# A two-layer transformer kernel: scores for the maxima in three passes, two filler banks, whole PSUM tiles in the planned part

## The chip, the core and the metric

The kernel runs on one core of one Trainium2 chip. The metric is device time in microseconds of one execution, as the median of three runs.

A core has a matrix engine (TensorE, PE in the profile; PEld is its weight load), a vector engine (VectorE, DVE), an activation engine (ScalarE, ACT), GpSimd (POOL) and a queue that starts transfers (SyncE, SP). Matmul results go to PSUM, which the kernel divides into eight banks of 512 fp32 columns on 128 partitions. DVE and ACT take them out from there; the program makes a matmul that writes a bank again wait for the bank's last reader.

## The reference

Input x has 2 x 1024 tokens of width 256. Two layers follow one another, each with attention and a gated FFN beside each other:

```python
xn = _layernorm(x)
x = x + _L0_attn_ref(xn, ...) + _L0_ffn_ref(xn, ...)
xn = _layernorm(x)
x = x + _L1_attn_ref(xn, ...) + _L1_ffn_ref(xn, ...)
```

Layer 0 has linear attention (features elu(q)+1 and elu(k)+1, one 16x16 state per head) and an FFN with ternary weights. Layer 1 has softmax attention with rotary positions, and an FFN whose weights are seen through Hadamard transforms. What matters here is layer 1's attention, 16 heads of width 16 in each of the two batches:

```python
q = apply_rope(q)
k = apply_rope(k)
attn = jnp.einsum('bhqd,bhkd->bhqk', q, k) * scaling
probs = jax.nn.softmax(attn, axis=-1)
out = jnp.einsum('bhqk,bhkd->bhqd', probs, v)
```

The softmax needs the maximum of each row of 1024 scores before the exponentials of that row.

## The kernel before, in words

**The planned part.** Layer 0, the first two layer norms of layer 1, the first heads and the first maxima (`search`, L1180) are not issued as they are written. `Plan` (L158) records each operation with what it needs; `Plan.emit` (L225) then makes a list for PE, DVE, ACT and POOL with costs (`cost`, L340) and with the numbers in `LEADS` (L48), one for each group of operations and engine, which are added to an operation's urgency. A needed element is looked up at a grain (`Pool`, L272): the PSUM pool has grain C = 512, so the list sees the two banks of a two-bank tile as two things. In the wide FFN pieces (`ffn0`, L728) one two-bank tile `pug` holds the up product in bank one and the gate product in bank two, eight fp32r matmuls each; a tanh on ACT reads the first bank.

**The loop** (L1332 on) is issued in the order in which it stands. It goes over 8 units; a unit is four heads of one batch. In unit u the exponentials and weighted sums of unit u and the maxima of unit u+1 are made together. A *burst* (`burst`, L1044) works four row groups of 32 rows of PE at a time. Two groups make scores with keys on partitions for the exponentials, in three passes of 512 columns: high part of q, low part of q, and minus the maximum (`weights_of`, L1100, tile `sce`). The other two make scores with queries on partitions for the next unit's maxima, in two passes of 512 columns (`scores_of`, L1053, tile `scm`). After a burst DVE reduces the two banks of `scm` to maxima (`scores_max`, L1064, one reduction of 1024 columns) and ACT takes the exponentials of the two banks of `sce` (1024 columns, tile `pr`).

A unit has 16 steps of two bursts. I call a *half* the stretch from the first matmul of one burst to that of the next. In the A half of a step the weighted sums of the step before follow the burst (`weigh`, L1121, four groups of columns, tile `po`). In the B half *filler* follows: pieces of the FFNs (`pug`, then `py`), of the Hadamard products (`pw`), of the output projections, the transposes of maxima (`put_peaks`, L1088) and of finished sums (`normalise`, L1136), and, in units 0, 2 and 4, the next heads (`heads_of`, L825): a projection `pqkv`, rotation on POOL and DVE, and transposes `pt` (`lay_out`, L844) that ACT and DVE take out as `qk_hi` and `ql`. `fill` (L1216) issues filler for a share of the filler that is left; `go_on` (L1227) gives out the steps that wait for a place, among them the DVE operations behind a finished `pug`, which come behind the next burst's reduction. The last unit has 16 bursts in which all four groups make scores for exponentials, in three passes.

PSUM: `pair` has two buffers of two banks (for `scm` and `sce`), `bank` has three buffers of one bank for all filler, `po` has one bank. Each burst needs both pairs.

Of the kernel before, what the change touches and what calls it, by code (L numbers as in the profile page):

```python
# [21 lines left out]
P = 128  # L22
# [3 lines left out]
NB = E // P  # L26
# [22 lines left out]
    "norm 0a": (1268, 1283, 1353, 1307),  # L49
    "norm 0b": (1266, 1278, 1247, 1252),  # L50
    "norm 1": (1210, 1162, 1187, 1148),
    "project 0": (1056, 1212, 1220, 1354),
    "project 1": (981, 1355, 1139, 1289),
    "state 0": (594, 645, 635, 642),
    "attend 0": (974, 935, 955, 963),
    "attend 1": (417, 552, 629, 461),
    "wuT0": (1187, 1197, 1154, 1169),
    "wgT0": (1364, 1352, 972, 1039),
    "wdT0": (535, 515, 586, 606),
    "piece 0": (460, 529, 461, 589),  # L60
    "piece 1": (1299, 1282, 1268, 1287),
    "piece 2": (1099, 767, 1229, 1058),
    "piece 3": (965, 967, 900, 942),
    "norm1 0": (889, 872, 881, 927),
    "heads 0": (969, 1023, 971, 1088),
    "norm1 1": (921, 944, 969, 1152),
    "heads 1": (951, 921, 937, 944),
    "search 0": (588, 645, 635, 630),
    "search 1": (692, 602, 631, 644),
    "search 2": (639, 616, 689, 676),  # L70
    "search 3": (1243, 1270, 1288, 1295),
    "norm 2": (568, 534, 523, 547),
    "norm 3": (948, 938, 972, 960),
    "project 2": (654, 696, 637, 632),
    "project 3": (572, 548, 504, 552),
    "state 1": (571, 611, 558, 597),
    "attend 2": (1173, 1369, 1172, 1236),
    "attend 3": (644, 574, 633, 573),
    "piece 4": (906, 1076, 609, 921),
    "piece 5": (1168, 1568, 1476, 1520),  # L80
# [278 lines left out]
def tile_two_layers(ctx: ExitStack, tc: tile.TileContext, a: dict, out: bass.AP):  # L359
# [15 lines left out]
    ps = open_pool(ctx, "ps", 1, C, space=PSUM)  # L375
# [3 lines left out]

    def pair(name):  # L380
        return ps.tile([P, 2, C], F32, tag="pair", name=name, bufs=2)

    def bank(name):
        return ps.tile([P, C], F32, tag="bank", name=name, bufs=3)

    po = ps.tile([P, C], F32, tag="po", name="po", bufs=1)
# [84 lines left out]
    def norm_T(src, dst, pause=0.0):  # L471
# [23 lines left out]
        for k in range(2):  # L495
            pt = bank("pt")
            for j in range(CT):
                tensor.transpose(pt[:, j * P : (j + 1) * P], xn[:, j, k * P : (k + 1) * P], ident)
            yield CT * P * TR, SOON
            (vector.tensor_copy if k else scalar.copy)(dst[:, k, :], pt)  # L500
            yield 0.0


    def ffn(cc, first, second, half_scale, scale, down, before_down):
# [4 lines left out]
        for e in range(NB):  # L509
# [20 lines left out]
            vector.scalar_tensor_tensor(h, pug[:, 1, :], scale(e), act, ALU.mult, ALU.mult)  # L530
            hid.append(h)
            yield 0.0
        before_down()
        for j in range(F // P):
            t = at // P + j
            cols = slice(j * P, (j + 1) * P)
            py = bank("py")[:, 0:D]
            for e in range(NB):
                tensor.matmul(py, lhsT=hid[e][:, cols], rhs=down[:, e, :], start=(e == 0), stop=(e == NB - 1))
                if e < NB - 1:  # L540
                    yield D * COL
            yield D * COL, SOON
            vector.tensor_add(xc[c][:, t, :], py, xc[c][:, t, :])
            yield 0.0
# [183 lines left out]
    def ffn0(cc, before_down, wide=False, by_pool=False):  # L728
# [20 lines left out]
        for e in range(0, NB, step):  # L749
# [25 lines left out]
            else:  # L775
                vector.scalar_tensor_tensor(act, pug[:, 1, :, :], sgd, act, ALU.mult, ALU.mult)
            acts.append(act)
# [3 lines left out]
        py = [bank("py")[:, 0:D] for _ in range(F // P)]  # L781
        for e in range(NB):
            if e == 1 and acts:
                split()
            for j in range(F // P):
                if state.plan and e == 0 and not wide:
                    plan.behind(pug)
                for s in range(2):
                    lhsT = hid[e][s][:, j * P : (j + 1) * P]
                    tensor.matmul(py[j], lhsT=lhsT, rhs=wd[:, e, :], start=(e + s == 0), stop=(e + s == NB))  # L790
                if (e, j) != (NB - 1, F // P - 1):
                    yield 2 * D * PASS
        yield 2 * D * PASS, SOON
        for j in range(F // P):
            t = at0 // P + j
            vector.tensor_add(xc[c][:, t, :], py[j], xc[c][:, t, :])
        yield 0.0
# [27 lines left out]
    def heads_of(b, gg, first=0, last=BT):  # L825
# [28 lines left out]
        def take_out(cols, pt):  # L854
            scalar.copy(thk[:, :, cols], pt)
            vector.tensor_tensor(tl[:, :, cols], pt[:, 0:2, :], thk[:, 0:2, cols], ALU.subtract)

# [9 lines left out]
        for i in range(first, last + 2):  # L867
# [4 lines left out]
            if i >= last:  # L872
                yield 0.0, LAST
                if i == last:
                    split_k(i - 1)
                    yield 0.0, PAIR
                continue
            c, j = divmod(b * BT + i, CT)
# [4 lines left out]
            for k in range(2):  # L883
# [7 lines left out]
                if k == 0:  # L891
                    yield 3 * P * COL
            yield 3 * P * COL, LAST
            if i > first:
                split_k(i - 1)
            yield 0.0, FIRST
# [5 lines left out]
            )  # L902
            cos, sin = (
# [46 lines left out]
    def hadamard_in(name, tag):  # L950
        eff = const.tile([P, 2, E], F32, tag=tag, name=f"eff_{name}")
        had[name] = eff
        for n in range(E // C):
            cols = slice(n * C, (n + 1) * C)
            raw = loaded.pop(0)
            for m in range(2):
# [8 lines left out]
                vector.tensor_scalar_mul(eff[:, m, cols], pw, su_ug[:, m : m + 1])  # L965
                yield 0.0

    def hadamard_down():
        wd1 = const.tile([P, NB, D], F32, tag="wC", name="wd1")
        had["wdT1"] = wd1  # L970
        for n in range(2):
            raw = loaded.pop(0)
            for i in range(2):
# [6 lines left out]
                vector.tensor_copy(wd1[:, e : e + 2, :].rearrange("p k n -> p (k n)"), pw)  # L980
                yield 0.0
# [62 lines left out]
    def burst(scores):  # L1044

        for s in range(max(len(passes) for _, passes in scores)):
            for sc, passes in scores:
                if s < len(passes):
                    tensor.matmul(
                        sc, lhsT=passes[s][0], rhs=passes[s][1], start=(s == 0), stop=(s == len(passes) - 1)  # L1050
                    )

    def scores_of(u, j, sc):  # L1053

        b, g = units[u]
        qt, r = divmod(j, 4)
        kh, p = divmod(r, 2)
        qs, ks = slice(qt * P, (qt + 1) * P), slice(kh * C, (kh + 1) * C)
        return [
            (sc[:, i, :], [(q[b, g][rows[2 * p + i], qs], kk[b, g][rows[2 * p + i], ks]) for q in (qh, ql)])  # L1060
            for i in range(2)
        ]

    def scores_max(u, j, sc):  # L1064
        qt, r = divmod(j, 4)
        kh, p = divmod(r, 2)
        n, t = divmod(qt, CT)
        if (u, n) not in peaks:
            peaks[u, n] = small.tile([P, CT, 2, 4], F32, tag="peak", name="peak")
        peak = peaks[u, n]  # L1070
        vector.tensor_reduce(peak[:, t, kh, 2 * p : 2 * p + 2], sc, AX.X, ALU.max, negate=True)
        if j % 16 == 15:
            nm = small.tile([P, CT, 4], F32, tag="nm", name="nm")
            vector.tensor_tensor(nm, peak[:, :, 0, :], peak[:, :, 1, :], ALU.min)
            if u == 0 and n == 1:
                nms.append(nm)
                return
            split_peaks(nm)
            if u > 0:
                later(2, lambda: put_peaks(u, n))  # L1080
# [7 lines left out]
    def put_peaks(u, n):  # L1088
# [7 lines left out]
        scalar.copy(mx[u][:, n * C : (n + 1) * C], pt)  # L1096
        left[0] -= CT * P * TR / 2
        spent[0] += CT * P * TR / 2

    def weights_of(u, i, p, sc):  # L1100

        b, g = units[u]
        n, r = divmod(i, 16)
        ks, qs = slice(r // 2 * P, (r // 2 + 1) * P), slice(n * C, (n + 1) * C)
        made = []
        for k in range(2):
# [3 lines left out]
                (sc[:, k, :], [(keys, qh[b, g][r, qs]), (keys, ql[b, g][r, qs]), (ones_r[r, :], mx[u][r, qs])])  # L1110
# [25 lines left out]
    def normalise(u, n, oT):  # L1136
# [13 lines left out]
        )  # L1150
        if g == NG - 1:
# [4 lines left out]
    def project(b, n):  # L1156
# [3 lines left out]
        pts = []  # L1160
        for k in range(2):
            pts.append(bank("pt"))
            for j in range(CT):
                tensor.transpose(pts[k][:, j * P : (j + 1) * P], att[b, n][:, j, k * P : (k + 1) * P], ident)
        yield 2 * CT * P * TR, SOON
        scalar.copy(aT[:, 0, :], pts[0])
        vector.tensor_copy(aT[:, 1, :], pts[1])
        yield 0.0
        parts_left[c] -= 1
        last = parts_left[c] == 0  # L1170
        for j in range(CT):
# [3 lines left out]
            vector.tensor_add(xc[c][:, j, :], py, xc[c][:, j, :])  # L1175
            if last:
                sync.dma_start(out=out_d[:, c * CT + j, :], in_=xc[c][:, j, :])
            yield 0.0

    def search(part):  # L1180

        for i in range(STEPS // 4):
            j = part // 2 * 16 + part % 2 * 2 + i // 2 * 4 + i % 2
            sc = pair("sc")
            plan.burst = True
            burst(scores_of(0, j, sc))
            plan.burst = False
            scores_max(0, j, sc)
            yield
# [37 lines left out]
    def go_on(*when):  # L1227
# [3 lines left out]
        if urgent and waits.get(urgent[0], 0) in when:  # L1231
# [73 lines left out]
    l0.close()  # L1305
    late.append(open_pool(ctx, "late", 2))
# [11 lines left out]
    slots = STEPS // 2  # L1318
    to_fill = [slots * (len(units) - 1) + slots / 2]
    pending = []  # L1320

    def slot(weight):
        share = max(left[0], 0.0) / to_fill[0] * weight
        to_fill[0] -= weight
        tick()
        fill(max(share - stage(), 0.0), filler)
        go_on(LAST)

    def keep(u, i, prs):
        pending.append((u, i // 16, i % 16 // 2, prs))  # L1330

    for u in range(len(units) - 1):  # L1332
# [9 lines left out]
        for i in range(0, STEPS, 2):  # L1342
            prs = []
            for p in range(2):
                scm, sce = pair("scm"), pair("sce")
                burst(scores_of(u + 1, i + p, scm) + weights_of(u, i, 1 - p, sce))
                scores_max(u + 1, i + p, scm)
# [93 lines left out]
```

## Time and profile before

| | us |
|---|---|
| median of 3 runs | 916.99 (913.85 to 917.79) |
| profiled execution, its own time | 912.87 |
| its span | 911.1 |
| first burst of the loop starts at | 216.0 |
| last maxima of the loop are reduced from | 845.8 |
| clock granted to PE, mean | 0.998 of full |

PE is busy for 95% of the span, DVE 64%, ACT 48%, POOL 24%. A line of the groups reads: line, engine, operation, out<-in, shapes, count, then busy time in total and mean ns of one, then idle time of the engine just ahead of these instructions and who ended it. All lines stand as L316, the helper through which every operation is issued, so the tile names tell the operations apart. A PE row's fp32 matmul counts as two instructions. In the timeline a row has its start, its length, engine, operation, count and, in brackets, how long the engine had been idle and what it waited for. Weight loads start a matmul: the time of a PEld row is when PE begins with it.

### The profile page before, as it was taken

Reading aid. Unit: us, or ns where it says so; the run is one execution under the profiler, and the core shown is the slowest. Engines: PE = TensorE matmul, PEld = TensorE weight load, DVE = VectorE, ACT = ScalarE, POOL = GpSimd, SP = SyncE. Lnnn points to the kernel's source line nnn. Section 1 sums busy time; section 2 is a strip of 40 time slices with the busy share of each in tenths; the row PEclk is TensorE's granted clock in tenths of the full one; section 3 lists DMA queues with packets and bytes.
Section 4 is the critical chain, followed back from the end, with each engine's and each line's share of the span. In section 5 each row is a group of like instructions: output and inputs, shape, how many; then the busy total and the mean of one; then the engine's idle time right before and its main releaser. Section 6 shows DMA issues by size and latency. Waiting matters only on the chain.

```text
span 911.1 us, 14625 instructions
## 1 busy us (share of the span) xinstructions
PE 868.0 (95%) x6064; PEld 518.4 (57%) x6064; DVE 584.2 (64%) x956; ACT 440.6 (48%) x641; POOL 214.7 (24%) x280
## 2 busy tenths in 40 slices
PE   8988999999989998999999999999999999999997
PEld 5677855676546543555555555555555555555543
DVE  5975557787876687656765656677565666656212
ACT  6534565433655543444544444455344444444563
POOL 2645589432643140004500000054000000000000
PEclk9999999999999999999999999999999999999999
DMA  8200000000000110000000000000000000000001
GB/s 304 75 1 1 2 0 1 1 2 1 1 24 25 47 47 0 1 1 1 1 2 1 1 1 25 1 1 2 24 1 1 1 1 1 1 1 1 1 7 40
DMA packets 11313, 14.77 MB, mean 16 GB/s; under 512 B 1264, under 2 KB 8944, under 8 KB 11248
## 3 DMA queue, kind: packets, MB, share of 16 engines
q1 hardware_dynamic: 11248, 13.85, 4.5%
q8 instruction: 47, 0.77, 0.4%
q14 instruction: 18, 0.15, 0.1%
HBM read 11.75 MB, written 2.10 MB: 15 GB/s over the span
## 4 chain that ended last, share of the span: by engine, by line
PE 69%; DVE 21%; ACT 4%; issue 2%; POOL 2%; DMA 1%; SPq 0%; ACTq 0%; POOLq 0%; DVEq 0%
PE pug L316 19%; DVE peak L316 16%; PE scm L316 16%; PE py L316 12%; PE sce L316 7%; PE pqkv L316 4%; PE pt L316 4%; PE pw L316 2%; PE sc L316 2%; PE po L316 2%; ACT pr L316 1%; ACT act L316 1%; DVE act L316 1%; DMA x<-in_x 1%; PE pq L316 1%
## 5 line engine op out<-in xcount | busy, mean ns | idle before, releaser
L316 ACT ACTIVATE pr<-sce 128x1024 f32<-128x1024 f32 x256 | 260.5, 1024 | 269.3 <-PE sce L316 269.0
L316 DVE TENSOR_REDUCE peak<-scm 128x2 f32<-128x1024 f32 x224 | 274.1, 1223 | 166.1 <-PE scm L316 165.2
L316 PE MATMUL po<-pr,va 128*17 128x512 f32 x1024 | 135.6, 598 | 0.0
L316 PEld LDWEIGHTS scm<-qk_hi 32*128 32x128 f32 x448 | 41.4, 181 | 151.1 <-DVE peak L316 113.6
L316 PE MATMUL sce<-qk_hi 32*128 32x512 f32 x512 | 122.6, 494 | 4.8 <-DVE peak L316 2.4
L316 PE MATMUL scm<-qk_hi 32*128 32x512 f32 x448 | 111.5, 494 | 11.8 <-DVE peak L316 1.0
L316 POOL CAST tops<-nm 128x16 fp32r<-128x16 f32 x16 | 3.4, 212 | 406.9 <-DVE nm L316 406.7
L316 PE MATMUL sce<-ql,qk_hi 32*128 32x512 f32 x512 | 97.0, 392 | 0.0
L316 PE MATMUL sce<-mx,ones_r 32*128 32x512 f32 x512 | 97.0, 391 | 0.1
L316 PE MATMUL scm<-qk_hi,ql 32*128 32x512 f32 x448 | 89.0, 394 | 0.0
L316 DVE SCALAR_TENSOR_TENSOR act<-act,pug 128x256 f32<-128x256 f32 (+1 forms) x112 | 50.8, 453 | 58.2 <-ACT act L316 35.1
L316 PE MATMUL pug<-xnT,eff_wgT 128*128 128x256 f32 x256 | 69.2, 392 | 0.0
L316 PE MATMUL pug<-xnT,eff_wuT 128*128 128x256 f32 x256 | 68.3, 382 | 0.0
L316 PE MATMUL py<-wd,hid 128*128 128x256 f32 x256 | 63.2, 388 | 0.0
L316 POOL TENSOR_TENSOR hid<-act,hid 128x256 fp32r<-128x256 f32 (+1 forms) x48 | 45.9, 956 | 70.1 <-ACT hid L316 42.3
L316 ACT ACTIVATE act<-pug,ws_ug 128x256 f32<-128x256 f32 x64 | 30.4, 475 | 55.4 <-PE pug L316 55.4
L316 PEld LDWEIGHTS pug<-xnT,eff_wgT 128*128 128x128 f32 x256 | 45.5, 189 | 16.6 <-issue 10.7
L316 PEld LDWEIGHTS py<-wd,hid 128*128 128x128 f32 x256 | 46.4, 190 | 14.8 <-issue 8.5
L316 PEld LDWEIGHTS sce<-qk_hi 32*128 32x128 f32 x512 | 45.8, 181 | 15.8 <-ACT pr L316 9.9
L316 PEld LDWEIGHTS pug<-xnT,eff_wuT 128*128 128x128 f32 x256 | 47.9, 190 | 9.8 <-issue 2.6
L316 PEld LDWEIGHTS sce<-mx,ones_r 32*128 32x128 f32 x512 | 46.3, 183 | 11.0 <-ACT mx L316 0.5
L316 ACT ACTIVATE act<-pug,su_half 128x256 f32<-128x256 f32 (+1 forms) x48 | 26.1, 546 | 52.1 <-PE pug L316 44.8
(146 smaller groups left out, 1337.6 us busy)
## 6 DMA issues: line engine op xcount, KB each, us to landing
out<-x SPq DMA_DIRECT2D x16, 128.0 KB, 1.7
x<-in_x SPq DMA_DIRECT2D x3, 512.0 KB, 9.4
both<-in_wuT SPq DMA_DIRECT2D x1, 1024.0 KB, 8.8
both<-in_wgT SPq DMA_DIRECT2D x1, 1024.0 KB, 10.4
wdT<-in_wdT SPq DMA_DIRECT2D x1, 1024.0 KB, 12.6
raw<-in_wdT SPq DMA_DIRECT2D x2, 512.0 KB, 4.2
raw<-in_wgT SPq DMA_DIRECT2D x2, 512.0 KB, 3.9
raw<-in_wuT SPq DMA_DIRECT2D x2, 512.0 KB, 3.4
```

Source lines behind the costliest of these rows:

```text
L316: return call(*map(real, args), **{k: real(v) for k, v in kw.items()})
```

## The change

1. In a burst the two groups that make scores for maxima now use all three pass times: their tile `scm` has three banks (`triple`), one head gets three quarters of 256 keys and the other two (turn about), each in two passes, so five quarters a burst in place of four. A matmul has 512 or 256 columns, since a quarter can lie across a bank's edge or a query block's end. Maxima are taken by two reductions, one for each head, the shorter first; in a unit there are 26 such bursts in 13 steps.
2. The three steps left over in a unit (`LOOKS`) have one burst each, all four groups making scores for exponentials into `sce` and `scf` (two banks of the `triple`). So a unit has 29 bursts in place of 32; the last still has 16.
3. PSUM in the loop: one `pair`, one `triple`, two banks `bank0` and `bank1` for filler, `po`. `bank(name)` takes the bank that was not taken last, unless it is held, and a bank is held from being taken until the operation that reads it last has been issued (`free`). A new pool is opened for this behind the planned part.
4. A halves get filler too (`FIRST_PART` = 0.4 us, behind the weighted sums). The heads' projection moves from ahead of the filler to behind it, just ahead of the next burst, and its DVE additions are issued at once. The FFN's down products and the output projection's transposes take one bank at a time.
5. The planned part sees a PSUM tile as a whole (grain 2C) and has new `LEADS`.

```diff
-    ps = open_pool(ctx, "ps", 1, C, space=PSUM)
+    psum = [open_pool(first, "ps", 1, 2 * C, space=PSUM)]
...
     def bank(name):
-        return ps.tile([P, C], F32, tag="bank", name=name, bufs=3)
...
+        k = 1 - last[0] if 1 - last[0] not in held else last[0]
+        assert k not in held, name
+        last[0] = k
+        held.append(k)
+        t = psum[1].tile([P, C], F32, tag=f"bank{k}", name=name, bufs=1)
...
             if i >= last:
-                yield 0.0, LAST
                 if i == last:
+                    yield 0.0, LAST
                     split_k(i - 1)
                     yield 0.0, PAIR
                 continue
+            yield 0.0, LAST
             c, j = divmod(b * BT + i, CT)
...
+    LOOK = [[(3, 2)[(i + k) % 2] if i < 12 else 2 for i in range(13)] for k in range(2)]
+
+    def look(u, p, i, sc):
+
+        flat = sc.rearrange("p b n -> p (b n)")
+        groups, maxima = [], []
+        for k, parts in enumerate(LOOK):
+
+            first, n = sum(parts[:i]), parts[i]
+            at = 0 if n == 3 or (n == LOOK[1 - k][i] and k == 0) else 2 * C
+            group, g = [], first
+            while g < first + n:
+                qt, a = divmod(g, S // F)
+
+                m = min(first + n - g, S // F - a, 2 - (g - first) % 2)
+                col = at + (g - first) * F
+                group += scores(u, 2 * p + k, qt, a * F, (a + m) * F, flat[:, col : col + m * F])
+                g += m
+            groups.append(group)
+            out_ = peaks_of(u)[:, 2 * p + k, :, :].rearrange("p q n -> p (q n)")[:, first : first + n]
+            maxima.append((out_, flat[:, at : at + n * F].rearrange("p (g n) -> p g n", g=n)))
+
+        def take():
+
+            for out_, in_ in sorted(maxima, key=lambda x: x[1].ids.size):
+                vector.tensor_reduce(out_, in_, AX.X, ALU.max, negate=True)
...
+    LOOKS = [i % 5 < 4 for i in range(2 * BT)]
+    ALONE = 0.4
+    FIRST_PART = 0.4
...
-    for u in range(len(units) - 1):
+    for u in range(len(units)):
...
-        for i in range(0, STEPS, 2):
+        m = 0
+        for i in range(2 * BT):
             prs = []
...
+            if LOOKS[i] and u < len(units) - 1:
+                us = share(1)
+                for p in range(2):
+                    scm, sce = triple("scm"), pair("sce")
+                    groups, take = look(u + 1, p, m, scm)
+                    burst(*weights_of(u, i, 1 - p, sce), *groups)
+                    take()
+                    prs.append(weights_exp(sce))
+                    if p == 0:
+                        go_on(SOON, FIRST)
+                        sums()
+                        fill(min(us, FIRST_PART), filler)
+                    else:
+                        go_on(SOON, SECOND)
+                        tick()
+                        rest = us - FIRST_PART - stage() - (6 * P * COL if urgent else 0.0)
+                        fill(max(rest, 0.0), filler)
+                        go_on(LAST)
+                prs.reverse()
+                m += 1
+            else:
+                scs = [pair("sce"), triple("scf")[:, 0:2, :]]
+                burst(*weights_of(u, i, 0, scs[0]), *weights_of(u, i, 1, scs[1]))
+                prs = [weights_exp(sc) for sc in scs]
+                go_on(SOON, FIRST, heads=False)
+                sums()
+                tick()
+                fill(share(ALONE), filler)
```

## The prediction

> **What bounds the kernel now.** The page first: busy shares, the chain that ended last, the costliest groups.
>
> ```profile
> PE 868.0 (95%) x6064; PEld 518.4 (57%) x6064; DVE 584.2 (64%) x956; ACT 440.6 (48%) x641; POOL 214.7 (24%) x280
> ...
> PE 69%; DVE 21%; ACT 4%; issue 2%; POOL 2%; DMA 1%; SPq 0%; ACTq 0%; POOLq 0%; DVEq 0%
> ...
> L316 DVE TENSOR_REDUCE peak<-scm 128x2 f32<-128x1024 f32 x224 | 274.1, 1223 | 166.1 <-PE scm L316 165.2
> ```
>
> PE sets the time, and the DVE part of the chain is mostly the maxima. So I read a plain step of the loop in the timeline.
>
> ```profile
> 503.66 0.49 PE L316 MATMUL scm<-qk_hi 32*128 32x512 f32 x2
> ...
> 503.99 0.40 PE L316 MATMUL scm<-qk_hi,ql 32*128 32x512 f32 x2
> ...
> 504.24 0.39 PE L316 MATMUL sce<-mx,ones_r 32*128 32x512 f32 x2
> 504.43 1.22 DVE L316 TENSOR_REDUCE peak<-scm 128x2 f32<-128x1024 f32 x1 [1.46 <-PE scm L316]
> 504.56 0.13 PEld L316 LDWEIGHTS po<-pr,va 128*17 128x17 f32 x8 [0.36 <-issue]
> ...
> 504.73 1.02 ACT L316 ACTIVATE pr<-sce 128x1024 f32<-128x1024 f32 x1 [0.49 <-PE sce L316]
> 505.57 0.41 DVE L316 SCALAR_TENSOR_TENSOR act<-act,pug 128x256 f32<-128x256 f32 x1
> 505.71 0.18 PEld L316 LDWEIGHTS scm<-qk_hi 32*128 32x128 f32 x2 [1.02 <-DVE peak L316]
> ...
> 506.02 0.48 DVE L316 SCALAR_TENSOR_TENSOR hid<-pug,ws_ug,act 128x256 f32<-128x256 f32 x1
> ...
> 506.70 0.73 PEld L316 LDWEIGHTS pug<-xnT,eff_wgT 128*128 128x128 f32 x4 [0.37 <-issue]
> ```
>
> From the burst's start: reduction at 0.77 (after two passes), next PE work at 0.90, exponential at 1.07, next burst at 2.05, when the reduction is over. The `pug` of the half before is free only at 2.84, when `hid` ends. Here nobody minds: the A half issues no filler. One half does mind (from its burst's start):
>
> ```profile
> 252.47 0.50 PE L316 MATMUL scm<-qk_hi 32*128 32x512 f32 x2
> ...
> 253.24 1.23 DVE L316 TENSOR_REDUCE peak<-scm 128x2 f32<-128x1024 f32 x1 [0.72 <-PE scm L316]
> ...
> 254.40 0.58 ACT L316 CAST qk_hi<-pt 128x512 fp32r<-128x512 f32 x1
> 255.01 0.42 DVE L316 TENSOR_TENSOR ql<-pt,qk_hi 128x256 fp32r<-128x256 f32 x1
> 255.49 1.56 PE L316 MATMUL pqkv<-wqkvT,xnT 128*128 128x384 f32 x4 [1.56 <-DVE ql L316]
> ```
>
> The projection waits for `ql` behind the reduction: the half takes 4.98 against about 3.3 for its work. Last, PE's waits ahead of the loop:
>
> ```profile
> PE pug L316 <- ACT act L316: 7.4, 10, 0.8
> ```
>
> That is the gate half of a wide `pug` standing behind the tanh that reads its other bank: a tile is waited for as a whole, though the list counts by bank.
>
> **The loop's work, part by part.** Prices from the timeline: burst 0.90; sums (`po`) to the next work 0.98 (849.01 to 849.99); change from filler to a burst 0.22 (eight `pug` instructions, 1.71 of streaming, take 1.93); an fp32 filler matmul 0.43, fp32r 0.12, projection matmul 0.64, transpose 0.11, Hadamard 0.85. Counted in the two built orders, filler costs 277 us in both and sums 128 x 0.98 in both. Bursts fall from 240 to 219: 21 x 0.90 = 19 saved. But some 90 A halves now carry filler and pay a change of 0.22: 20 lost. So PE's work stays.
>
> Waits for the maxima. Before: an A half is 2.05 against 1.88 of work, 111 x 0.17 = 19 us, and the B burst behind it is drawn out to 0.99, 10 more. After: `scm` is one tile, and in the built order only the first of the two reductions waits for PE, so I let both start when the whole burst is over, at 1.02. A reduction of 512 columns is 0.69 (the row of a 128x512 copy out of PSUM), 768 is 0.96 between that and 1.22, and DVE starts the next 0.08 early: through at 2.59, burst at 2.65. An A half with one fp32 filler matmul has 0.90 + 0.98 + 0.43 + 0.22 = 2.53 of work: 58 halves x 0.12 = 7; some B halves too short for 2.65 add 7, drawn-out bursts 5. Together 19 after, 29 before: 10 gained. If the short reduction starts at 0.77, 12 more.
>
> Matmuls of 256 columns. [...] I take 0.03 a burst: 5 us, between 0 and 31.
>
> **The new wait.** Filler has two banks, and A halves use them. I walked through the built order with the banks: where is a bank taken in the half in which its last reader is issued, which on DVE stands behind both reductions? Before, five halves (work beyond price: 1.68, 0.58, 0.29, 0.80, 0.72). After, 46 in the loop ahead of the tail. A second count agrees: bursts whose `scm` needs no DVE wait of its own, since filler of the half before has waited for a later DVE instruction, are 5 before and 52 after (without those behind a lone burst).
> - A half, 13 times: the new `pug` gets the bank of the one just done. `act`, `hid` end at 2.59 + 0.41 + 0.48 - 0.04 = 3.44, PE starts at 3.5 where it arrives at 1.88; the half is 4.15, not 2.65: 13 x 1.45 = 19.
> - B half, 25 times: mostly transposes `pt`, then `pqkv` in the same bank. `rot` and `ql` end near 3.35; PE arrives at 1.8 to 2; then 1.28 and 0.22: 4.9 or a little less against 3.3: 25 x 1.5 = 37.
> - B half, 8 times twice in a row (`hid`, then `pt`, then `ql`, then `pqkv`): 6.4 against 3.3: 25.
> Sum 81, less 4 that these waits cost before: 77. Behind the waiting matmul stand, in order, the rest of the filler and the next burst, so ACT and DVE wait too and nothing fills the gap. Bounds: nothing, if the readers are done when PE arrives; 92, if all 52 take the mean of these 46 (1.76). I keep 77, since the one half of the trace that shows this chain paid its full price (1.68).
>
> **The rest.** Lone bursts: 2.87 by two exponentials (1.94 and 0.9, as in the last unit), 3.2 of work: no wait; the pair that the next burst needs is free by then. Ahead of the loop: whole tiles take away the 7.4, the new order makes other waits that I can't price by a row; -11 (all that PE idles there from 50 us on by the stage table: 7.6 from 50 to 100, 2.7 to 150, 0.8 to 216) to +5, I take -5, since a part of such stalls comes back as waits for something else. Maxima's final minimum, 14 reductions of 64 elements near 0.2 (before 0.17): hidden on DVE. The heads' additions `qk` and `va` (0.41 and 0.28) now stand ahead of the next burst's reductions; the projection ends about 0.2 behind that burst's start, so they are through by 0.9, ahead of 1.02: nothing, and 0.15 in 24 halves if reductions could start at 0.77. The rotation on POOL starts earlier for it. The single banks of the down products and of the output projection are in the walk above. SP keeps its work; output transfers follow the same additions. The new PSUM pool waits once for the last readers: under 1. The tail (15 us) is the same chain.
>
> Sum: 0 - 10 + 5 + 77 - 5 = +67 on a span of 911.1: 978, with 1.8 around it 980. The profiled run lay 4.1 below the median, so 984.
>
> **Rivals.**
> - Faster: the readers are early. If both reductions start at pass ends and DVE lets `act`, `hid`, `ql` through by 1.9 us, the waits are nought: -10 - 12 + 5 - 7 = -24, 893. For it: DVE is busy 64%. Against: program order puts them behind the reductions. It decides at a mean wait of 24/52 = 0.46 us. Chance 0.06.
> - Half price: short reduction at 0.77 and PE later than I count, so 46 waits of 0.85, near what the cheaper ones of before cost: 39 - 4, with -22 + 5 - 5 a gain of 13 to set on 917: 930. Chance 0.12, from 915 to 945.
> - Same: these gains and losses cancel, within 0.5% (about what a measurement can tell from no change): 0.04.
> - [...] Chance 0.08.
> - Forecast, 945 to 1005: 0.70. The range takes in half of the half price and the nearer half of the dear case: 930 to 1015, with some 0.8 in it. Slower in all 0.90.
>
> **What would show it.** First burst between 205 and 221; 172 or so short and 168 long reductions near 0.69 and 0.96, the short one 1.02 (not 0.77) behind its burst; A halves of 2.65 and of 4.15; waits of `pqkv` on `ql` near 1.5 and of `pug` on `hid` near 1.6, 70 to 80 us in all where before had 4; PE's share below 90%. If those waits stay under 25 us in all, I am wrong on the main step; if passes of 256 columns stretch bursts past 1.05, on the load.

## The result, and the profile after

The changed kernel takes 994.47 us (median of 4 runs, 991.49 to 996.15) where before takes 916.34 in the same comparison: ratio 1.085 (1.081 to 1.089), 78 us slower. The forecast was 984, in a range of 930 to 1015. The profiled execution took 995.89 us (span 994.1), so the lines below are of a typical run.

The page of the changed kernel, the same rows that the prediction began with:

```profile
PE 897.8 (90%) x6400; PEld 553.0 (56%) x6400; DVE 586.4 (59%) x1096; ACT 436.6 (44%) x641; POOL 209.2 (21%) x280
...
PEclk9999999997789999999989999989899999999999
...
PE 77%; DVE 16%; ACT 4%; issue 2%; DMA 1%; SPq 0%; POOL 0%; ACTq 0%; DVEq 0%
...
L316 DVE TENSOR_REDUCE peak<-scm 128x2 f32<-128x512 f32 x364 | 279.4, 809 | 207.0 <-PE scm L316 168.1
```

PE's share falls from 95% to 90% and DVE's from 64% to 59%: the engines wait more. The reductions cost 279 us in place of 274, so DVE has no new work. PE's busy time rises from 868 to 898 us, though the kernel has 21 bursts fewer. Most of that rise can be the clock. The row PEclk has sevens and eights where before had only nines, and the mean granted clock is 0.965 in place of 0.998. In the loop PE works for 59.5 us at half its clock, where before it was 3.4 us.

In the timeline, the first burst of the loop starts at 204.99 in place of 216.04. From there to the start of the last burst it is 774.2 us in place of 680.2: 94 us more, of which the earlier start gives 11 back; the rest behind the last burst (15 us) is the same.

The waits of PE in the changed kernel (engine, tile, who was waited for: total, times, longest):

```profile
PE pug L316 <- DVE hid L316: 16.6, 10, 2.1
PE pqkv L316 <- DVE ql L316: 12.9, 14, 1.6
PE pt L316 <- DVE act L316: 10.8, 4, 2.9
PE pug L316 <- DVE act L316: 9.1, 5, 2.2
```

All rows of filler tiles (`pug`, `pqkv`, `pt`, `py`, `pw`) that wait for another engine within the loop come to 75.1 us in 54 waits; before has 3.9 us in 6. One A half of this kind, in the timeline of the changed kernel:

```profile
463.91 0.50 PE L316 MATMUL sce<-qk_hi 32*128 32x512 f32 x2
...
464.02 0.47 ACT L316 ACTIVATE act<-pug,ws_ug 128x256 f32<-128x256 f32 x1 [0.47 <-PE pug L316]
...
464.61 0.27 PE L316 MATMUL scm<-qk_hi,ql 32*128 32x256 f32 x1
...
464.81 1.05 PE L316 MATMUL po<-pr,va 128*17 128x512 f32 x8
464.96 1.56 DVE L316 TENSOR_REDUCE peak<-scm 128x2 f32<-128x512 f32 x2 [3.63 <-PE sce L316]
...
466.43 0.41 DVE L316 SCALAR_TENSOR_TENSOR act<-act,pug 128x256 f32<-128x256 f32 x1
466.88 0.48 DVE L316 SCALAR_TENSOR_TENSOR hid<-pug,ws_ug,act 128x256 f32<-128x256 f32 x1
...
467.42 0.70 PE L316 MATMUL pug<-xnT,eff_wgT 128*128 128x256 f32 x2 [1.55 <-DVE hid L316]
468.05 0.18 PEld L316 LDWEIGHTS sce<-qk_hi 32*128 32x128 f32 x2 [0.33 <-issue]
```

The two reductions, one right behind the other, start 1.05 behind the burst's start. `act` and `hid` (the readers of the bank that the filler needs next) stand behind them, and the filler starts at 3.51. The half takes 4.14. The bracket behind DVE's reduction shows the other side of it: DVE had been idle for 3.63 us. The readers could not have used all of that, since ACT's tanh on this `pug` ends at 464.49, 0.47 ahead of the reductions. In that time `act` (0.41) would have been done, and `hid` would have put the reductions off by some 0.4 (an estimate: 0.41 + 0.48 less the 0.47).

### The profile page after: what moved, and what is told of

It reads as the page before. It is cut to its first block, busy times and chain, and to the rows that moved or that the text cites. A ratio compares the mean times of both kernels' runs of the same rounds, so it can differ in the third digit from the quotient of the medians.

```text
span 994.1 us, 15578 instructions
## 1 busy us (share of the span) xinstructions
PE 897.8 (90%) x6400; PEld 553.0 (56%) x6400; DVE 586.4 (59%) x1096; ACT 436.6 (44%) x641; POOL 209.2 (21%) x280
## 4 chain that ended last, share of the span: by engine, by line
PE 77%; DVE 16%; ACT 4%; issue 2%; DMA 1%; SPq 0%; POOL 0%; ACTq 0%; DVEq 0%
PE pug L316 18%; PE sce L316 14%; PE py L316 11%; PE po L316 10%; DVE peak L316 8%; PE scm L316 6%; PE pqkv L316 6%; PE pt L316 3%; PE pkv L316 2%; ACT pr L316 2%; PE pw L316 2%; DVE act L316 2%; PE scf L316 1%; PE sc L316 1%; PE pq L316 1%
## 5 line engine op out<-in xcount | busy, mean ns | idle before, releaser
L316 DVE TENSOR_REDUCE peak<-scm 128x2 f32<-128x512 f32 x364 | 279.4, 809 | 207.0 <-PE scm L316 168.1
L316 ACT ACTIVATE pr<-sce 128x1024 f32<-128x1024 f32 x219 | 224.1, 1023 | 359.4 <-PE scm L316 173.1
L316 PE MATMUL scm<-qk_hi 32*128 32x256 f32 (+1 forms) x616 | 144.8, 393 | 2.0 <-DVE peak L316 1.6
L316 PE MATMUL scm<-qk_hi,ql 32*128 32x256 f32 (+1 forms) x616 | 121.1, 331 | 0.0
L316 PE MATMUL sce<-qk_hi 32*128 32x512 f32 x438 | 111.9, 507 | 1.6 <-ACT pr L316 1.4
L316 PE MATMUL pug<-xnT,eff_wgT 128*128 128x256 f32 x256 | 76.1, 409 | 18.6 <-DVE hid L316 16.6
L316 PE MATMUL sce<-mx,ones_r 32*128 32x512 f32 x438 | 87.8, 395 | 0.1
L316 PEld LDWEIGHTS scm<-qk_hi,ql 32*128 32x128 f32 x616 | 81.3, 188 | 6.3
L316 PEld LDWEIGHTS scm<-qk_hi 32*128 32x128 f32 x616 | 79.1, 186 | 7.5 <-issue 4.3
L316 PE MATMUL pqkv<-wqkvT,xnT 128*128 128x384 f32 x128 | 66.2, 648 | 16.8 <-DVE ql L316 12.9
L316 PE MATMUL pug<-xs,t_wuT 128*128 128x256 f32 x256 | 44.8, 307 | 10.4 <-DVE act L316 9.1
## 6 DMA issues: line engine op xcount, KB each, us to landing
wdT<-in_wdT SPq DMA_DIRECT2D x1, 1024.0 KB, 12.4
```

The source lines that it names most:

```text
L316: return call(*map(real, args), **{k: real(v) for k, v in kw.items()})
```

## Theories and experiments

My theory, from the prediction: with two banks, filler takes a bank in the half in which its last reader is issued, and that reader stands behind the reductions. Rivals: the bursts themselves (256 columns, third pass, late reductions) cost the time; the filler put into A halves does; the planned part's gain is only work pushed into the loop. Before took 912.8 to 913.9 in the comparisons below; ratios are to before of the same comparison.

**e1: the loop of the change, the planned part of before.**

```diff
-    psum = [open_pool(first, "ps", 1, 2 * C, space=PSUM)]
+    psum = [open_pool(first, "ps", 1, C, space=PSUM)]
...
+LEADS of before
```

> The changed kernel with the planned part of before: grain C and the old LEADS; the loop is that of the change. If the planned part gives 11 us of its own (first burst at 205 against 216), this one is at about 1005, its first burst near 216, and the loop stays at 774. If the earlier first burst is only work pushed into the loop, the first burst is near 216 and the loop shorter by the same 11, so that the time stays at 994.

1008.83 us, ratio 1.106 (1.100 to 1.112). First burst at 217.38 (the change: 204.99), from first to last burst 770.5 (the change: 774.2). So the planned part's gain of 12.4 us is its own: the loop pays back 3.7 of it at most. By the ratios the two kernels lie 19 us apart, more than the traces show; the granted clock differs between e1's runs (0.961 to 0.972), and the trace has 0.972.

**e2 and e3: the bursts of before with two filler banks, and with three.**

```diff
-    LOOK = [[(3, 2)[(i + k) % 2] if i < 12 else 2 for i in range(13)] for k in range(2)]
+    LOOK = [[2] * 16 for k in range(2)]
...
-    LOOKS = [i % 5 < 4 for i in range(2 * BT)]
+    LOOKS = [True for i in range(2 * BT)]
...
-        return psum[-1].tile([P, 3, C], F32, tag="triple", name=name, bufs=1)
+        return psum[-1].tile([P, 2, C], F32, tag="triple", name=name, bufs=1)
...
-        k = 1 - last[0] if 1 - last[0] not in held else last[0]
+        k = next(k for k in ((last[0] + d) % 3 for d in (1, 2, 3)) if k not in held)
```

(The last pair of lines is e3 alone. Both also give each head's maxima a bank of their own, and wait with the transposes of the maxima for the last burst that they need.)

> The changed kernel with the bursts of before: each head gets two quarters of maxima a burst, in two passes of 512 columns, 16 steps of two bursts and no lone burst; the second tile is two banks, and filler keeps its two banks (one bank is left unused). If the shortage of banks costs the time, this is about as slow as the changed kernel, 990 to 1015, since its bank reuses are as many (64 against 62 by the order). If three passes, 256 columns and the late start of the reductions cost it, this drops to 925 to 945.

> As e2_two_banks, with the eighth bank given to filler, taken in turn: 17 reuses are left in place of 64. Nothing else differs. If banks are the cause, 60 us or more below e2_two_banks: 930 to 950, granted clock back near 1.0, waits of pqkv on ql and of pug on hid under 20 us together. If not, within 15 us of e2_two_banks.

e2: 992.74, ratio 1.087 (1.083 to 1.090). e3: 920.06, ratio 1.007 (1.005 to 1.010). One bank is worth 72.7 us, in kernels that issue the same operations (6064 on PE and 1180 on DVE in both), and e2, without third pass, lone bursts and 256 columns, is as slow as the changed kernel. e3 came 10 us below its expectation. The clock goes with it: 0.974 in e2, 0.991 in e3. Waits of filler in the loop: 75.3 us in 63 waits, against 24.5 in 19. So some 51 of the 72.7 us are waits. Most of the rest can be the clock: PE works at half its clock for 49.8 us of the loop in e2 and for 16.9 in e3, which is worth up to 16 us (an estimate: half of the difference).

**e4: readers ahead of the reductions.** One line in the changed kernel:

```diff
                     burst(*weights_of(u, i, 1 - p, sce), *groups)
+                    go_on(SOON, heads=False)
                     take()
```

> The changed kernel with one edit: the readers of a finished filler bank are issued ahead of the two reductions instead of behind them. 35 reuses behind reductions are left of 62, nearly all pt to pqkv of the heads. If order behind the reductions is the cause: 30 to 50 us less, 945 to 965, waits of pug on hid below 12 us, those of pqkv on ql unchanged near 30. If the reductions bound the halves, what now stands ahead of them makes every such half longer by 0.3: 1010 to 1025.

955.66, ratio 1.046 (1.042 to 1.050): 36 us less than the change by the ratios (0.039 x 913). A half's readers now run ahead of the reductions, for the most part while DVE waits for the burst; the first reduction moves from 1.06 to 1.23 behind its burst (medians). Waits of filler in the loop fall from 75 to 42 us. The waits of PE in e4:

```profile
PE pqkv L316 <- DVE ql L316: 19.7, 18, 1.6
PE pug L316 <- DVE hid L316: 4.3, 2, 2.1
```

`pug` on `hid` falls from 16.6 to 4.3. `pqkv` on `ql`, which the edit doesn't touch, stays (12.9 before, 19.7 now). So it is the order on DVE, and not the number of banks by itself, that makes a bank expensive.

**e5 and e6: the kernel before with the new planned part, and with e4's line on top.**

```diff
-    ps = open_pool(ctx, "ps", 1, C, space=PSUM)
+    ps = open_pool(ctx, "ps", 1, 2 * C, space=PSUM)
...
+LEADS of the change
...
                 burst(scores_of(u + 1, i + p, scm) + weights_of(u, i, 1 - p, sce))
+                if filler and waits.get(filler[0], 0) == SOON:
+                    step(filler)
                 scores_max(u + 1, i + p, scm)
```

(The last lines are e6 alone.)

> The kernel before with the planned part's grain 2C and the new LEADS; its loop is untouched. If the planned part gains by itself what e1_old_front lost by going back (12 us), the first burst is near 204 and the time 899 to 904. If the gain needs the changed loop, within 4 us of before.

> e5_new_front with the readers of a finished filler bank issued ahead of the burst's reduction, in the loop of before. If such readers only ever help, 4 us below e5_new_front, what the five waiting halves cost. If the reduction bounds the A halves of before (2.05 of 1.88), readers that end at about 1.3 us push it from 0.77 to 1.3 in the 60 or so A halves behind a finished pug: 15 to 30 us above e5_new_front.

e5: 899.31, ratio 0.985 (0.984 to 0.987); first burst at 202.02 instead of 216.04, loop 679.5 instead of 680.2. The planned part alone makes the kernel 13.5 us faster. e6: 932.27, ratio 1.020 (1.017 to 1.022), 33 us above e5. The line that gained 36 us in the changed kernel loses 33 in the loop of before: its A halves carry no filler, so nobody waits for the bank, and the readers only delay the reduction, for which the next burst waits. The waits of PE on the maxima, in e6 and then in e5:

```profile
PE scm L316 <- DVE peak L316: 41.0, 52, 0.9
PE sce L316 <- DVE peak L316: 2.7, 1, 2.7
```

```profile
PE sce L316 <- DVE peak L316: 2.4, 2, 2.2
...
PE scm L316 <- DVE peak L316: 1.0, 2, 0.8
```

The waits of `scm` on the reduction rise from 1.0 to 41.0 us. An A half goes from 2.065 to 2.38 on average (264.1 us in 111, 229.2 in e5).

**e7: e4 with the heads in another order.** The projection `pqkv` goes to the A half, and its additions and the taking out of `pt` go ahead of the next reductions. The core of the edit:

```diff
-                    go_on(SOON, heads=False)
+                    go_on(SOON, TAKE)
                     take()
...
                         sums()
-                        fill(min(us, FIRST_PART), filler)
+                        part = 0.0 if urgent else FIRST_PART
+                        go_on(SUMS)
+                        fill(min(us, part), filler)
```

> e4_early, and the heads in another order: the projection pqkv is issued in the A half behind the sums, its additions and the taking out of pt stand ahead of the next burst's reductions, so that pt and pqkv no longer follow one another in one bank within a half. 10 reuses behind reductions are left of 62, with two banks, triple and three passes as in the changed kernel. If bank order is the whole loss, 40 us below e4_early: 905 to 925, clock above 0.99. If the bursts of the third pass cost too, it stays above 930.

928.53, ratio 1.017 (1.015 to 1.020): 26 us less than e4, clock 0.989. Together with e4, 62 us of the changed kernel's loss go away by order alone (1.085 to 1.017), with two banks and all its bursts kept. Waits of filler in the loop are 24.9 us. It did not reach the expected 905 to 925 though; the 24.9 us of waits that are left are a part of that, and e8 asks whether the bursts are another.

**e8: the bursts of e2 in e7.** The edit is that of e2.

> e7_early_heads with the bursts of e2_two_banks (two quarters a head, 240 bursts, no lone burst), so that only the third pass differs from e7_early_heads, with hardly a bank wait in either. If the third pass is worth its 21 bursts, e8 is 10 to 20 us above e7. If the longer reductions and the late start eat that, the two are within 6 us or e8 is the faster.

918.08, ratio 1.006 (1.005 to 1.007): e8 is faster by 10 us. The third pass loses: it saves 21 bursts (19 us) and costs 29. Not all of the 29 is the bursts' own, since waits of filler come to some 25 us in e7 and 16 in e8; e9 settles what the bursts have to do with it.

**e9: two tiles instead of `triple`.**

```diff
-                    scm, sce = triple("scm"), pair("sce")
+                    scm, sce = (triple("scm"), one("scn")), pair("sce")
...
-            at = 0 if n == 3 or (n == LOOK[1 - k][i] and k == 0) else 2 * C
+            at = 0
+            flat = sc[0].rearrange("p b n -> p (b n)") if n == 3 or (n == LOOK[1 - k][i] and k == 0) else sc[1]
```

(`triple` now has two banks, `one` has one.)

> e7_early_heads with the three banks for maxima as two tiles: two banks for the head with the longer part, one for the shorter, so that each reduction waits for its own head's matmuls. If the third pass loses to e8_two_quarters because reductions chained from 1.02 on bound its halves (2.65), the shorter one now starts at about 0.77, the bound falls to 2.4, under the work of an A half (2.5), and the time to 900 to 912, below e8. If the third pass loses by its bursts (256 columns, more weight loads), it stays at 920 to 930.

911.77, ratio 0.998 (0.996 to 1.000), 17 us below e7 and 6 below e8. Its waits of filler are those of e7 (some 25 us). The shorter reduction now starts 0.81 behind its burst (median), instead of 1.19 in e7. So the third pass lost by its reductions, not by its matmuls. A burst of e7 in the timeline shows how:

```profile
564.33 0.95 DVE L316 TENSOR_REDUCE peak<-scm 128x3 f32<-128x768 f32 x1
...
565.15 0.50 PE L316 MATMUL sce<-qk_hi 32*128 32x512 f32 x2
...
565.42 0.50 PE L316 MATMUL scm<-qk_hi 32*128 32x512 f32 x2
...
566.40 1.56 DVE L316 TENSOR_REDUCE peak<-scm 128x2 f32<-128x512 f32 x2 [1.12 <-PE scm L316]
```

The first matmul on `sce` is free to start, that on `scm` waits until the reduction of 768 columns is over at 565.28, and the burst is drawn out by 0.27; its reductions start 1.25 behind it. Summed over the loop from the timelines, the time from a burst's start to the next work of PE is 46 us above 0.90 each in e7, 16 in e8 and 30 in e9.

**e10: e3 without filler in the A halves.**

```diff
-    FIRST_PART = 0.4
+    FIRST_PART = 0.0
```

> e3_three_banks without filler in the A halves (FIRST_PART 0). 109 changes from filler to a burst at 0.22 go (24 us), and the A halves, 1.88 of work, are bound by the two reductions: 0.77 + 2 x 0.69 + 0.06 = 2.2, 0.14 more than before's 2.065 (15 us above e5_new_front). So 905 to 915 if the change is what filler in A halves costs; 920 or more if e3 is above e5 for another reason (the order of the heads).

895.57, ratio 0.980 (0.978 to 0.982), 24.5 us below e3, and the fastest kernel of the study: the planned part of the change, three banks, two quarters a head, filler in the B halves only (51 A halves still finish a piece). Its mean A half is 2.42, the B half 3.21. It came 9 us below the expected range, whose own sum (e3 less 24) gave 896: I had added 15 us for A halves bound by the reductions. Only 60 A halves have the sums alone, and these take 2.14 (median) against 2.05 in e5, which makes 5 us.

**e11: e2 with PE kept busy in its waits.**

```diff
         held.append(k)
+        if k in behind[0]:
+            for _ in range(5):
+                tensor.matmul(behind[1][:, 0:P], lhsT=ident, rhs=ident, start=True, stop=True)
```

> e2_two_banks with five matmuls of 128 columns that nobody reads (about 1.1 us) into its unused bank, just ahead of each filler piece that takes a bank whose last reader stands behind this half's reductions: 72 places, 77 us of extra matmul work inside the waits. If the waits cost a second time through the granted clock, the clock goes from 0.974 towards 0.99 and the time falls by 5 to 15 us below e2_two_banks in spite of the extra work. If the clock has nothing to do with the waits, the clock stays at 0.974 and the time is the same or up to 30 us more, where a wait was shorter than 1.1.

986.02, ratio 1.080 (1.078 to 1.082), against 1.087 (1.083 to 1.090) for e2: 6.7 us less with 360 matmuls more. Granted clock 1.000, and the loop falls from 774.6 to 761.9 us, while five of the 72 places lie behind the last burst and lengthen the rest from 15 to 19 us. The rows of the granted clock, e2 first, then e11:

```profile
PEclk9999999999899999999799999999999999999999
```

```profile
PEclk9999999999999999999999999999999999999999
```

So at least 13 us of e2's loop are not waits but the slow clock that follows them. It can be more, since the matmuls put in hold PE for longer than the waits that they take away: some 80 us in the loop, where waits of filler fall by 61 (75.3 to 14.0).

**e12: before with the new LEADS alone,** the list still counting by bank.

> The kernel before with the new LEADS alone; the list still counts PSUM by bank (grain C), the loop is untouched. If the new numbers give what e5_new_front gained (13.5 us, ratio 0.985), the time is 899 to 903 and the first burst near 203. If seeing tiles as a whole is what takes the waits of the gate half on the tanh away (7.4 us on PE before, none in e5_new_front), those waits stay at 5 us or more and the time is 905 or above.

925.45, ratio 1.012 (1.010 to 1.014); first burst at 222.68, and 3.0 us of `pug` waits on the tanh are left, less than the 5 I had named. The new numbers without the whole tiles cost 11 us: the 13.5 of e5 need the two together. The order as such need not be what costs them. The granted clock is 0.979 to 0.983 in all five runs (before: 0.994 to 0.998), and in the stage table of e12 it is down around the loop's start:

```profile
150.00:216.00 66.00, 60.88 (x347) 43.51 (x344) 50.38 (x92) 17.33 (x40) 26.53 (x38) 0.87 0.00 1
216.00:300.00 84.00, 77.38 (x555) 45.13 (x553) 59.29 (x100) 41.27 (x66) 33.17 (x49) 0.92 0.05 14
```

(The columns are those of the last section's table; the clock is the number ahead of the last two.) The loop, whose program is that of before, takes 686.1 in place of 680.2. PE works for 33 us at half its clock, 3.4 in before, which is worth up to 15 us (an estimate). What the whole tiles give with the old numbers wasn't measured.

## Why the forecast held, point by point

The kernels make a chain in which each link is a part of the change, or a few parts together, all against about 913 for before (the change as 1.0852 x 912.9 = 990.7):

| from | to | part | us measured | us forecast |
|---|---|---|---|---|
| before 912.9 | e5 899.3 | planned part | -13.5 | -5 |
| e5 899.3 | e10 895.6 | order of the heads, two reductions, single banks | -4 | 0 |
| e10 895.6 | e3 920.1 | filler in A halves | +24.5 | +20 |
| e3 920.1 | e2 992.7 | third filler bank gone | +72.7 | +77 |
| e2 992.7 | changed 990.7 | third pass, lone bursts, 256 columns | -2 | -24 |

The last forecast is -19 for bursts, -10 for waits on maxima, +5 for 256 columns. The forecast's sum is +67 or +68, the measured one +78. The 10 us between them are what is left of misses of -8.5, -4, +4.5, -4 and +22. That these cancel as far as they do is luck; that the largest part came out as the largest is not.

- **The new wait: right in its place and in its sum.** Forecast: 70 to 80 us of such waits where before had 4. Measured: 75.1 against 3.9. Forecast for an A half with a bank just freed: filler from 3.5, half 4.15; measured 3.51 and 4.14. B halves with heads and one reuse were put at 4.9; those with one wait on `ql` and a full clock came at 4.81 to 5.07. B halves with two reuses in a row were put at 6.4, and the six longest B halves took 7.8 to 9.2, with the clock at half in them for 3.4 us or more. e3 against e2 puts the bank at 72.7, near the forecast's 77, but that is two things: 51 us of waits and, for most of the rest, the clock. The other 21 us of the waits came with the filler in A halves.
- **The clock: left out.** The forecast has no term for it. In the loop PE works at half clock for 56 us more than in before, which can be up to 28 of the loop's 94 us (an estimate: half of it). e11, with most of the waits filled, has a granted clock of 1.000 where e2 has 0.974, so the waits bring it about.
- **Waits for maxima: wrong.** The step "19 after, 29 before: 10 gained" failed. The prices in it were right (0.69 and 0.95 measured for the reductions, the first at 1.06 in the median), though the short ones are 196 and not 172. But I let PE's work of 2.53 in an A half hide a chain of 2.65 and booked the rest as 0.12. e7 shows what happens at that edge: the burst starts with `sce` and stands at `scm`, and its own reductions start later by as much, so the delay goes on to the next half. In bursts at full clock, the time to the next work of PE beyond 0.90 is 34 us in the changed kernel and 21 in before: 13 lost, where drawn-out bursts were to fall from 10 to 5. PE's visible waits ahead of bursts did fall, from 16 to 6 us. Between e7 and e8 the third pass costs 10 where the step and its neighbours gave -24. The remark beside it, 12 us if the short reduction starts early, was 17 in e9.
- **The loop's work: right in its sum, not shown in its cause.** 0.22 a change from filler to a burst gave 20; e3 against e10 gives 24.5 for 109 halves. But from e10 to e3 the waits of filler in the loop rise by 21 us, PE's busy time by 16 (of which the clock can be up to 7), and the waits ahead of bursts fall by 11. So the match with 0.22 is at least in part luck.
- **256 columns: right, with a term that no run shows.** The forecast's sum takes 5 us for these matmuls, 0.03 a burst, and bounds it by 31; no run shows either figure. What the runs show in their place: the median time from the burst to the sums in A halves is 0.90 in the changed kernel as in before (0.90), so weight loads of more passes are not seen to lengthen a burst. In before, passes of one row group start 0.25 apart (503.99, 504.24), and 16 fp32r matmuls of 256 columns start 0.118 apart (1.89 us from 61.24 on), so that two of these take 0.24.
- **The planned part: right in sign, outside its bounds.** The step "-11 (all that PE idles there from 50 us on by the stage table)" failed: e5 gained 14.0 to the first burst. PE's time without work ahead of the first burst fell from 18.1 to 9.3 us, within the bound, and its busy time fell as well, from 197.9 to 192.7, which I had taken as fixed. The two orders have the same number of matmul rows there (1180), so I read it as waiting inside busy rows; which matmuls had it, no run here separates.
- **The rivals.** "Faster" needed the readers through by 1.9 us. e4 made some of them so and gained only 36 us, since the waits of the heads and the third pass remained. The dear case (chance 0.08) needed longer bursts, and their median to the sums is 0.90 in both kernels. None of the chances was for what e10 shows: that two parts of the change, kept apart from the rest, are a gain.

## What to carry to other kernels

In the changed kernel the filler's matmul started 0.06 us after its bank's last reader had ended (467.42 behind `hid`, over at 467.36), and that reader ran where the program had put it in DVE's order, behind 1.56 us of reductions. So before giving up a buffer, list for each use what is queued ahead of the last reader, and move the reader or keep the buffer. The same move (reader ahead of the reduction) gained 36 us where PE waited for the buffer and lost 33 where PE waited for the reduction, so ask first which of the two is waited for last. When a change bundles parts, rebuild it as a chain of kernels: here one part was worth -13.5 us and hid under +78.

## What was not expected of the hardware

A wait on PE cost again in what followed it. The stage table of the changed kernel in steps of 2 us (columns: PE, PEld, DVE, ACT, POOL busy, then PEclk, the granted clock, then DMA):

```profile
224.00:226.00 2.00, 0.87 (x12) 0.61 (x10) 1.90 (x7) 1.63 (x3) 1.05 (x2) 1.00 0.00 0
226.00:228.00 2.00, 0.48 (x5) 0.52 (x6) 1.66 (x4) 0.00 (x0) 0.86 (x2) 1.00 0.00 0
228.00:230.00 2.00, 1.39 (x7) 0.88 (x7) 0.42 (x1) 0.78 (x2) 0.46 (x1) 0.62 0.00 0
230.00:232.00 2.00, 2.00 (x4) 0.66 (x2) 0.00 (x0) 0.00 (x0) 0.00 (x0) 0.50 0.00 0
232.00:234.00 2.00, 2.00 (x19) 1.51 (x22) 0.85 (x3) 0.21 (x1) 1.22 (x2) 0.50 0.00 0
234.00:236.00 2.00, 2.00 (x12) 0.53 (x4) 1.40 (x3) 1.38 (x3) 0.96 (x2) 0.68 0.00 0
```

PE waits 2.65 us up to 227.51 (`pt` on `act`), does transposes and half a `pug`, waits 0.61 for `ql`, and runs at half its clock from 228.5 to 235.3. A projection takes 2.92 us, and the burst behind it:

```profile
232.04 0.79 PE L316 MATMUL sce<-qk_hi 32*128 32x512 f32 x2
...
233.62 1.85 PE L316 MATMUL po<-pr,va 128*17 128x512 f32 x8
```

It takes 1.58 from the burst to the sums instead of 0.90, and 1.85 for sums that take 1.05.

The record of the clock is regular in the trace of the changed kernel: the stretches at half clock begin a multiple of 3.41 us apart, and the 15 in its loop last 3.41 or 6.83 us. So I cut the loops of before and of the changed kernel into pieces of 3.41 us, in step with that record, and added up PE's idle time in each that has the full clock. In the 16 pieces ahead of a fall (one of them in before) it was 1.29 to 2.65 us. In the other 389 it was at most 1.65, but in 15 of these 1.28 or more, so the idle time of a piece does not by itself tell here whether the clock falls; and the ends of matmuls are modelled. One piece ahead of a fall in e2, where the only wait is 2.02 us of `pug` on `hid`, and the piece behind it:

```profile
502.20:505.61 3.41, 1.39 (x13) 0.86 (x10) 2.10 (x4) 1.32 (x2) 0.00 (x0) 1.00 0.00 0
505.61:509.02 3.41, 3.41 (x16) 2.20 (x15) 0.00 (x0) 0.47 (x1) 0.00 (x0) 0.50 0.00 0
```

In the changed kernel two waits, of 0.91 and 0.65 us, preceded the fall at 706.33. That the waits bring the clock down is shown by e11, which fills most of them (75.3 to 14.0 us in the loop) and has 1.000 where e2 has 0.974; what else it takes, no run here shows.
